# A reciprocal of 128 x 512 softmax denominators issued as two of 128 x 256, in a convolution and attention kernel

## The chip, the cores and the metric

The kernel runs on one core of one Trainium2 chip. The metric is the time of one execution on the device in microseconds (us). Four runs of the kernel before gave 3142.19, 3145.72, 3148.43 and 3150.03 us; their median is 3147.07 us.

## The reference, cut to what matters

The input x has four images of 128 channels and 64 x 64 pixels, in f32. Layer 0 adds to x the output of a block that normalises x in groups of channels, sums three convolutions (7x7, 5x5, 3x3), adds a non-local attention and applies a ReLU. Layer 1 reads the pixels as 4096 tokens per image, adds a state-space mixer that runs forwards and backwards over the tokens, and then a recurrence with a sigmoid. Only the attention of layer 0 is touched:

```python
g_x = conv1x1(x, gw, gb).reshape(B, IC, hw)
theta = conv1x1(x, tw, tb).reshape(B, IC, hw)
phi = conv1x1(x, pw, pb).reshape(B, IC, hw)
f = jnp.einsum('bcn,bcm->bnm', theta, phi) / jnp.sqrt(jnp.float32(IC))
attn = jax.nn.softmax(f, axis=-1)
out = jnp.einsum('bcm,bnm->bcn', g_x, attn)
```

IC is 64 and hw is 4096. The softmax needs, for each of the 4096 queries n, the sum over all keys of exp(f). The kernel divides by that sum at the end, on the output.

## The kernel before, in words

The activations stay in one tile `t` of 128 channels x 16384 pixels in SBUF. Layer 0 (`conv_attention`) goes through 32 query tiles of 512 pixels, eight for each image, in one loop over n (L627). It fills roughly the first 1660 us of the span; the mixer and the recurrence of layer 1 fill the rest.

One query tile has two parts. In the first, an inner loop (L639) goes eight times over four blocks of keys. `scores` (L454) multiplies keys and queries on TensorE into PSUM (`pf`) and takes the exponential on ScalarE (`ex`, L462). `values` (L466) multiplies the exponentials with the values into a PSUM tile `acc` (L471), and VectorE adds the exponentials up into the SBUF tile `es` (L475, L477). Behind the loop L651 folds the two halves of `es` into one of 512 columns.

In the second part the generator `convolve` (L375) does the tile's share of the convolutions. It multiplies transformed pixels `yf` with transformed weights `wt` or `wc` on TensorE (`products`, L355, matmuls at L367), four or six groups one after the other, each into a PSUM tile `pm`. VectorE and ScalarE combine them (L410 to L420), GpSimd adds them further (L426, L432, L433, L437, L438 and `put`, L380) and makes the next pixels (`transform` and `forms`: L298, L337, L347). At the second yield of `convolve` the loop calls `divide` (L479): a matmul with a matrix of ones (L481) sums `es` over the partitions, so that all 128 rows of the PSUM tile `den` hold the 512 denominators; VectorE takes the reciprocal into the SBUF tile `att` (L483), notes its largest and smallest value (L484, L485, from one partition) and multiplies `acc` with it (L486). Between these steps the loop issues `queries` for the next tile (L449), and in the last tile of an image the `keys` of the next image (L259). `collect` (L489) projects `att` and adds it to `t`.

Three PSUM buffers under the tag "c" are shared by everything small: `pm`, `den`, `pt` (queries), `pc` (collect), `pp`, `pg` and `gt` (keys). A new tile under this tag waits until the last reader of the tile that held its buffer is done. In most tiles of the loop a `pm` two places behind `den` takes over the buffer of `den`, and so its first matmul waits for L483.

The order on TensorE and ScalarE is the order in which the program is written (L232). The order on VectorE, GpSimd and the transfer queues is set by a scheduler that works with estimated durations. In the built program a reciprocal is followed on VectorE by L484 and L485, in some tiles with one L414 ahead of them; nothing stands between L483 and what it waits for, the matmul L481.

A reciprocal of another size occurs once more in the code that runs, at L1042 in the mixer: 128 x 256 from SBUF to SBUF.

Of the kernel before, what the change touches and what calls it, by code (L numbers as in the profile page):

```python
# [17 lines left out]
NC = 512  # L18
# [135 lines left out]
def conv_attention(nc, tc, k, a, t, B, H, W, flags, load, mem, loads):  # L154
# [32 lines left out]
    with ExitStack() as ctx:  # L187
# [291 lines left out]
        def divide(n, acc, es):  # L479
            den = ps_c.tile([P, NC], F32, tag="c", name="den")  # L480
            nc.tensor.matmul(den, k.ones, es[:, 0, :], start=True, stop=True)  # L481
            att = wk.tile([P, NC], F32, tag="att", name="att", bufs=4)
            nc.vector.reciprocal(att, den)  # L483
            nc.vector.tensor_reduce(dmax[:, n : n + 1], att[0:1, :], AX.X, ALU.max)  # L484
            nc.vector.tensor_reduce(dmin[:, n : n + 1], att[0:1, :], AX.X, ALU.min)  # L485
            nc.vector.tensor_tensor(att, acc, att, ALU.mult)  # L486
            return att
# [139 lines left out]
        for n in range(N):  # L627
# [25 lines left out]
            for i, _ in enumerate(convolve(n, b, m, f, wts)):  # L653
# [9 lines left out]
                if i == 1:  # L663
                    atts[n] = divide(n, acc, es)
# [1089 lines left out]
```

## Time and profile before

| what | value |
|---|---|
| median of four runs | 3147.07 us |
| the profiled execution's own time | 3142.8 us |
| its span | 3141.1 us (1.7 us lie around it) |
| granted TensorE clock, mean over the span | 0.981 |
| TensorE busy, 500 to 900 us | 389.58 of 400 us |
| VectorE busy, 500 to 900 us | 276.20 of 400 us |
| GpSimd busy, 500 to 900 us | 243.77 of 400 us |
| ScalarE busy, 500 to 900 us | 169.56 of 400 us |
| reciprocal L483 | 32 times, 107.4 us in all |

The page of the profile lists busy time by engine, the span in 40 slices, the chain of work that ended last, and groups of equal instructions with the idle time of their engine ahead of them. PE is TensorE, PEld its weight loads, DVE VectorE, ACT ScalarE, POOL GpSimd, SP the queue of the transfers. A wait is written as who waited, an arrow, and who ended the wait.

### The profile page before, as it was taken

Reading aid. Unit: us, or ns where it says so; the run is one execution under the profiler, and the core shown is the slowest. Engines: PE = TensorE matmul, PEld = TensorE weight load, DVE = VectorE, ACT = ScalarE, POOL = GpSimd, SP = SyncE. Lnnn points to the kernel's source line nnn. Section 1 sums busy time; section 2 is a strip of 40 time slices with the busy share of each in tenths; the row PEclk is TensorE's granted clock in tenths of the full one; section 3 lists DMA queues with packets and bytes.
Section 4 is the critical chain, followed back from the end, with each engine's and each line's share of the span. In section 5 each row is a group of like instructions: output and inputs, shape, how many; then the busy total and the mean of one; then the engine's idle time right before and its main releaser. Section 6 shows DMA issues by size and latency. Waiting matters only on the chain. (4 is left out here: it accounts for less than half of the span.)

```text
span 3141.1 us, 42863 instructions
## 1 busy us (share of the span) xinstructions
PE 2936.4 (93%) x15511; PEld 1458.3 (46%) x15511; DVE 2197.1 (70%) x3429; ACT 1815.6 (58%) x3102; POOL 1803.8 (57%) x1394
## 2 busy tenths in 40 slices
PE   6899999999999999999997999999999999999976
PEld 2345444454444454444453444444444444455545
DVE  7876668666677667677765767677677767677667
ACT  3343334434344433444434878887788778888756
POOL 4258448456584655766552565555555665555644
PEclk9999999999999999999998999999999999999988
DMA  5310101010100101011023343334333343334332
GB/s 182 133 40 29 38 31 45 8 44 23 46 23 30 43 23 38 31 53 36 8 80 88 95 115 92 98 95 115 85 99 92 90 110 98 95 98 101 87 109 109
DMA packets 108394, 224.16 MB, mean 71 GB/s; under 512 B 25678, under 2 KB 29390, under 8 KB 106764
## 3 DMA queue, kind: packets, MB, share of 16 engines
q1 hardware_dynamic: 96588, 177.53, 20.2%
q10 hardware_dynamic: 11584, 43.78, 4.1%
q8 instruction: 125, 2.05, 0.3%
q14 instruction: 97, 0.79, 0.1%
HBM read 200.83 MB, written 20.44 MB: 70 GB/s over the span
## 5 line engine op out<-in xcount | busy, mean ns | idle before, releaser
L477 DVE TENSOR_TENSOR es<-es,ex 128x1024 f32<-128x1024 f32 x448 | 685.3, 1530 | 133.6 <-ACT ex L462 100.0
L462 ACT ACTIVATE ex<-pf 128x1024 f32<-128x1024 f32 x512 | 497.6, 1022 | 461.0 <-PE pf L460 418.1
L460 PE MATMUL pf<-theta,phi 64*128 64x512 f32 x2048 | 512.8, 618 | 20.4 <-ACT ex L462 19.9
L471 PE MATMUL acc<-ex,gT 128*64 128x512 f32 x2048 | 490.3, 605 | 1.7 <-ACT ex L462 1.7
L1202 POOL TENSOR_TENSOR ct<-ct,Cst 128x512 f32<-128x512 f32 x128 | 169.9, 1327 | 395.2 <-DMA ct<-csmem 372.8
L460 PEld LDWEIGHTS pf<-theta,phi 64*128 64x128 f32 x2048 | 173.0, 185 | 339.4 <-ACT ex L462 173.8
L1168 ACT ACTIVATE lt<-lt,cs 128x128 f32<-128x128 f32 x1024 | 312.2, 390 | 0.5 <-DMA lt<-csmem 0.5
L367 PE MATMUL pm<-yf,wt 128*128 128x256 f32 x1152 | 287.1, 382 | 11.9 <-DVE att L483 11.0
L410 ACT ACTIVATE eo<-pm 128x256 f32<-128x256 f32 x88 | 33.8, 384 | 448.7 <-PE pm L367 442.2
L471 PEld LDWEIGHTS acc<-ex,gT 128*64 128x64 f32 x2048 | 127.2, 136 | 337.6 <-issue 325.7
L367 PEld LDWEIGHTS pm<-yf,wt 128*128 128x128 f32 x1152 | 212.9, 189 | 93.4 <-issue 38.7
L1103 PE MATMUL pb<-tl,wbc_fwd 128*64 128x512 f32 x512 | 237.6, 607 | 2.8 <-DVE xT L1135 2.8
L1103 PE MATMUL pb<-tl,wbc_bwd 128*64 128x512 f32 x512 | 238.2, 607 | 0.0
L337 POOL TENSOR_TENSOR yf<-yd 128x272 f32<-128x272 f32 x192 | 236.0, 1257 | 1.4
L1267 POOL TENSOR_TENSOR yT<-yT,zT 128x512 f32<-128x512 f32 x127 | 170.3, 1349 | 35.7 <-DVE yT L1254 32.9
L337 POOL TENSOR_TENSOR yf<-xp 128x272 f32<-128x272 f32 x128 | 108.8, 881 | 129.7 <-PE pm L367 123.9
L1201 DVE TENSOR_TENSOR lt<-lt,gm 128x1024 f32<-128x1024 f32 x128 | 178.9, 1398 | 1.9
L1135 DVE SCALAR_TENSOR_TENSOR xT<-px,taps_bwd,xT 128x512 f32<-128x512 f32 x192 | 143.8, 749 | 8.9 <-ACT xT L1129 4.0
L1234 PE MATMUL y<-lt,xdt 128*64 128x128 f32 x2048 | 141.2, 280 | 4.4 <-PE ptr L1177 4.0
L1103 PEld LDWEIGHTS pb<-tl,wbc_fwd 128*64 128x64 f32 x512 | 65.8, 138 | 164.2 <-issue 137.4
L1221 POOL TENSOR_TENSOR S<-S,tot 128x256 f32<-128x256 f32 x120 | 91.3, 761 | 84.7 <-PE y L1242 83.2
L367 PE MATMUL pm<-yf,wc 128*128 128x256 f32 x512 | 131.2, 384 | 6.6 <-DVE att L483 5.1
(297 smaller groups left out, 5678.3 us busy)
## 6 DMA issues: line engine op xcount, KB each, us to landing
lt<-csmem SPq DMA_DIRECT2D x128, 512.0 KB, 5.7
wt<-wd ACTq DMA_DIRECT2D x72, 576.0 KB, 3.8
ct<-csmem SPq DMA_DIRECT2D x256, 128.0 KB, 5.3
rs<-m SPq DMA_DIRECT2D x31, 512.0 KB, 3.6
wd<-t SPq DMA_DIRECT2D x16, 576.0 KB, 2.8
t<-in_x SPq DMA_DIRECT2D x4, 2048.0 KB, 10.9
rows<-after SPq DMA_DIRECT2D x32, 256.0 KB, 4.8
out<-t SPq DMA_DIRECT2D x4, 2048.0 KB, 14.4
```

What stands on the lines that cost most here:

```text
L337: nc.gpsimd.tensor_tensor(f[:, kx], at(x), at(y), op)
L367: nc.tensor.matmul(pm[:, e, :], wt, src, start=(i == 0), stop=(i == len(terms) - 1))
L460: nc.tensor.matmul(pf[:, e, :], phi[HALF[e], m, :], th[HALF[e]], start=True, stop=True)
L462: nc.scalar.activation(ex, pf, AF.Exp, scale=scale)
L471: nc.tensor.matmul(acc[HALF[e]], gT[:, 2 * m + e, :], ex[:, e, :], start=(m == 0), stop=(m == NT // 2 - 1))
L477: nc.vector.tensor_tensor(es, es, ex, ALU.add)
L1103: nc.tensor.matmul(out, w[i]["bc"][:, tap, bass.ts(c, DS)], src, start=(tap == 0), stop=(tap == KC - 1),)
L1135: nc.vector.scalar_tensor_tensor(at(n), px, taps[:, PAD - n : KC - n], at(n), ALU.mult, ALU.add)
L1168: nc.scalar.activation(v, v, AF.Relu, scale=-1.0, bias=m["b"]["cs"][:, d, m["i"], h : h + 1])
L1201: nc.vector.tensor_tensor(lt, lt, gm.unsqueeze(2).to_broadcast([P, ND, NHEAD, P]), ALU.mult)
L1202: nc.gpsimd.tensor_tensor(m["ct"], m["ct"], Cs[:, cols].unsqueeze(1).to_broadcast([P, NHEAD, P]), ALU.mult)
L1267: eng.tensor_tensor(v, v, gr["z"][d][:, :, half(d, j // 2)], ALU.mult)
```

## The change

The one reciprocal of 128 x 512 becomes two of 128 x 256, over the left and the right half of the columns. Everything else in the source is as it was.

```diff
             den = ps_c.tile([P, NC], F32, tag="c", name="den")
             nc.tensor.matmul(den, k.ones, es[:, 0, :], start=True, stop=True)
             att = wk.tile([P, NC], F32, tag="att", name="att", bufs=4)
-            nc.vector.reciprocal(att, den)
+
+            for i in range(2):
+                nc.vector.reciprocal(att[:, bass.ts(i, NC // 2)], den[:, bass.ts(i, NC // 2)])
             nc.vector.tensor_reduce(dmax[:, n : n + 1], att[0:1, :], AX.X, ALU.max)
             nc.vector.tensor_reduce(dmin[:, n : n + 1], att[0:1, :], AX.X, ALU.min)
             nc.vector.tensor_tensor(att, acc, att, ALU.mult)
```

In the built program the order of the instructions on VectorE, TensorE, ScalarE and the transfer queues is otherwise the same; the two halves stand one behind the other, and the second has no wait of its own. On GpSimd five additions L426 change places with the L347 behind them, one L337 moves ahead by a few places, and one small L74 moves by one. On TensorE 26 first matmuls of a `pm` now wait for two things, VectorE and TensorE's own earlier matmul `den`; one instruction holds one of these waits, so that 25 waiting instructions (event semaphores) are new on its queue.

## The prediction

> **What bounds the kernel now.** I read the page first, its busy times and its 40 slices. Each slice is 78.5 us, so slices 2 to 21 are the loop over the 32 query tiles, in which the change lies.
>
> ```profile
> PE 2936.4 (93%) x15511; PEld 1458.3 (46%) x15511; DVE 2197.1 (70%) x3429; ACT 1815.6 (58%) x3102; POOL 1803.8 (57%) x1394
> ...
> PE   6899999999999999999997999999999999999976
> ...
> DVE  7876668666677667677765767677677767677667
> ```
>
> TensorE (PE) is busy over nine tenths of nearly every slice of the loop, VectorE (DVE) six or seven. The loop goes at TensorE's pace, and VectorE counts only where TensorE stands still for it. So the second view is the list of waits of TensorE alone from 96 to 1650 us; its columns are the total in us, the count, and the longest.
>
> ```profile
> PE pm L367 <- DVE att L483: 16.1, 19, 0.8
> PE pf L460 <- ACT ex L462: 11.7, 33, 1.8
> PE gt L280 <- ACT g L276: 8.5, 12, 0.9
> ```
>
> The largest wait in the list is the one on the reciprocal: 19 tiles, 16.1 / 19 = 0.85 us each. The third view, the timeline of one such tile, shows what it is.
>
> ```profile
> 141.91 1.02 PE L481 MATMUL den<-es,ones 128*128 128x512 f32 x2
> ...
> 142.96 3.36 DVE L483 RECIPROCAL att<-den 128x512 f32<-128x512 f32 x1 [0.17 <-PE den L481]
> ...
> 144.49 1.04 PE L449 MATMUL pt<-xp,tw 128*128 128x512 f32 x2
> ...
> 146.24 0.36 DVE L414 SCALAR_TENSOR_TENSOR eo<-pm,eo 128x256 f32<-128x256 f32 x1
> 146.38 0.73 PEld L367 LDWEIGHTS pm<-yf,wc 128*128 128x128 f32 x4 [1.70 <-DVE att L483]
> 146.38 1.13 PE L367 MATMUL pm<-yf,wc 128*128 128x256 f32 x4 [0.85 <-DVE att L483]
> ...
> 149.34 0.69 DVE L418 TENSOR_TENSOR eo<-eo,pm 128x512 f32<-128x512 f32 x1 [0.64 <-PE pm L367]
> ```
>
> The reciprocal ends at 142.96 + 3.36 = 146.32; the matmul that takes over the PSUM buffer of `den` starts at 146.38, 0.06 later. So in 19 tiles the path runs from `den` through the whole reciprocal back to TensorE, and each ns by which the reciprocal ends later is lost. What it delays on VectorE itself is covered: at 149.34 VectorE sits 0.64 us waiting for TensorE.
>
> In the other 13 tiles TensorE does not wait for L483. In eight of them each `pm` group has eight matmuls and not four, and TensorE comes to the buffer later: in the tile at 285.74 the reciprocal ends at 289.10 and the weight load of the next `pm` starts at 289.44, a cover of 289.44 - 289.10 - 0.06 = 0.28 us. In three (448.85, 851.70, 1254.89) a weight load for L267 waits 0.33 us for L485 behind the reciprocal. The first tile (96.14) waits for ScalarE afterwards, and the tile at 1502.85 for nothing of VectorE.
>
> **What the change removes, adds and moves.** It removes 32 reciprocals of 128 x 512 and adds 64 of 128 x 256. Nobody can start earlier: L484, L485 and L486 read all 512 columns, and the buffer of `den` is free only when both halves have been read. So there is no gain in the source; it is a matter of what the split costs. The groups by form give both sizes:
>
> ```profile
> L483 DVE RECIPROCAL att<-den 128x512 f32<-128x512 f32 x32 | 107.4, 3358 | 5.8 <-PE den L481 5.7
> L1042 DVE RECIPROCAL u<-u 128x256 f32<-128x256 f32 x4 | 7.0, 1747 | 1.8 <-ACT xe L1041 1.8
> ```
>
> Half the columns take 1747 ns and not 1679: the line through both rows is 3358 - 1747 = 1611 ns for 256 columns plus a fixed 1747 - 1611 = 136 ns. L1042 reads SBUF and L483 PSUM. The nearest row for a PSUM source is L246, a copy of one column, at 158 ns in all; with that as the fixed part a half is (3358 - 158) / 2 + 158 = 1758 ns. I take 1747.
>
> Between two halves there may be overlap. The second waits for nothing; how VectorE runs two such instructions is seen in the mixer, L1135, alternating between two tiles that do not depend on each other, and in the tile above:
>
> ```profile
> 1703.87 0.74 DVE L1135 SCALAR_TENSOR_TENSOR xT<-px,taps_fwd,xT 128x512 f32<-128x512 f32 x1
> 1704.53 0.74 DVE L1135 SCALAR_TENSOR_TENSOR xT<-px,taps_bwd,xT 128x512 f32<-128x512 f32 x1
> ```
>
> The second starts 0.66 us after the first, which lasts 0.74: 0.08 us overlap. L414 at 146.24 starts 0.08 ahead of the end of the reciprocal as well, so a reciprocal in front allows it. Where the second does depend on the first, it starts about 0.04 later than its end (L1042 ends at 1691.06 + 1.75 = 1692.81, L1043 starts at 1692.85).
>
> - Reciprocal, as I take it: 2 x 1.747 - 0.08 - 3.358 = **+0.056 us** a tile. Lower bound: no fixed part at all and overlap, 2 x 1.679 - 0.08 - 3.358 = -0.08. Upper bound: fixed part of L246 and no overlap, 2 x 1.758 + 0.04 - 3.358 = +0.198.
> - TensorE's queue: in the built program the `pm` that waits for L483 now has two conditions, VectorE and its own earlier matmul `den`. The second is long met (`den` has ended before the reciprocal starts), but the VectorE condition now stands in a waiting instruction of its own ahead of the matmul: 26 more at L367 and one fewer at L83. The rows of L367 list 102 such instructions, 51 ns at the least and in the median. Where the wait ends the idle time that is **+0.051 us**. Lower bound 0 (the queue covers it); upper bound 0.051 plus a second restart of 0.06 as above, 0.11.
> - GpSimd: five L426 and the L347 behind them change places (in the runs before at about 194, 514, 917, 1320 and 1415 us). L426 comes 1.2 us later, L347 1.2 us earlier. No wait of TensorE for GpSimd is in its list, and the results of L426 there are read by L432 or L437 a tile later. I take 0; if that cover were gone it is 1.2 us each way, five times.
>
> Sum on the path: 19 x (0.056 + 0.051) = **+2.0 us**. The eight tiles with eight matmuls hide 0.11 behind their 0.28 us, and the three with `keys` lose at most 3 x 0.1. The profiled execution took 3142.8 us (span 3141.1), so its counterpart is 3144.8. It is 4.3 us below the median of the four runs, and the loss is one of fixed durations, so it goes on the median: 3147.07 + 2.0 = 3149.1, predicted **3149**.
>
> [...]
>
> **The rivals.**
>
> - *Slower, by an exposed second half.* The second reciprocal starts only when the first is out of the pipeline, its start-up is that of a PSUM read, and TensorE restarts twice: 0.198 + 0.11 = 0.308 us a tile. With the three `keys` tiles that is 22 x 0.308 = 6.8 us: 3153.9, +0.22%. It decides from 6.3 / 22 = 0.29 us a tile. For it: two reciprocals in a row are nowhere in the trace. Against it: the overlap behind L483 itself.
> - *Nothing lost.* The halves cost 1.68 each and overlap, and the queue hides its wait: between 19 x (-0.08) = -1.5 and 0 us, 3145.6 to 3147.1. Against it: L1042 at 1747.
> - *Faster, through GpSimd.* With L347 earlier the next pixels `yf` are ready earlier. If each of five L347 and the one L337 that moves were on the path, it is 6 x 1.2 = 7.2 us: 3139.9, -0.23%. Against it: TensorE's waits name no GpSimd, and GpSimd itself waits 123.9 us for TensorE to free `yf`.
> - *The change does not do what it says.* The halves stand as two instructions in the built program, so this falls out.
>
> **How the numbers follow.** The forecast gets 0.64, nothing lost 0.20, the slower rival 0.10, the faster one 0.06. A measurement of this kernel can tell about 0.2%, 6.3 us, from no change; the first two cases lie within that: same 0.84, slower 0.10, faster 0.06. The range takes in the first three cases, 3145.6 to 3153.9, and 2 us at each side for the median of a few runs that lie between 3142.2 and 3150.0: 3143.5 to 3156.
>
> **What would show it.** Right: 64 rows of L483 near 1747 ns, the second starting 0.08 us ahead of the first one's end; TensorE's wait for L483 still in 19 tiles, at about 0.96 us each, 18 us in all; 128 waiting instructions at L367. Wrong: halves well over 1.76 us or a gap between them; a TensorE wait of over 1.1 us, or one in the eight-matmul tiles; a new wait of TensorE for `yf` or `eo` of GpSimd.

## The result and the profile after

The changed kernel takes 3150.36 us (median of 35 runs, 3145.02 to 3158.01), the kernel before 3146.82 us beside it (57 runs, 3139.31 to 3154.43). The ratio is 1.0013, with a 95% interval of 1.0008 to 1.0018: 4.1 us slower, between 2.5 and 5.7 (the two medians lie 3.5 us apart). That is within 0.2%, as forecast, and on the side that was forecast; against these runs the sum of 2.0 us was too small. A repetition in another set of runs (e1 below) gave 1.0003, 0.9994 to 1.0013, which is 0.9 us and does not exclude 0 or 2.0 us.

The groups by form of the kernel after show the two halves, 107.8 us in all where the one reciprocal took 107.4. The view of L485 shows that the 64 are of two kinds (columns: shortest, median, longest, in ns).

```profile
L485 DVE RECIPROCAL att<-den 128x256 f32<-128x256 f32 x64 | 107.8, 1726 | 5.8 <-PE den L481 5.7
```

```profile
L485 DVE RECIPROCAL att<-den x64: 1694/1726/1759, 96.5 to 1649.6; 128x256 f32<-128x256 f32 x64
```

The timeline, asked for each half of the tile shown before by itself, says which is which:

```profile
143.18 1.76 DVE L485 RECIPROCAL att<-den 128x256 f32<-128x256 f32 x1 [0.17 <-PE den L481]
```

```profile
144.85 1.70 DVE L485 RECIPROCAL att<-den 128x256 f32<-128x256 f32 x1
```

The first half takes 1759 ns, the second 1694, and the timeline gives 3.37 us for both together. So the second starts 1.759 + 1.694 - 3.37 = 0.08 us ahead of the end of the first, as forecast, and is itself 0.065 us shorter. TensorE's list of waits, again from 96 to 1650 us:

```profile
PE pm L367 <- DVE att L485: 18.1, 19, 1.0
PE pf L460 <- ACT ex L462: 12.2, 33, 2.3
PE gt L280 <- ACT g L276: 8.5, 12, 0.9
PE pv L252 <- DVE qv L250: 4.6, 3, 1.6
```

The same 19 tiles wait, 18.1 us and not 16.1, the very figure that was forecast; but the timeline of the tile shown before has it from another place:

```profile
143.18 3.37 DVE L485 RECIPROCAL att<-den 128x256 f32<-128x256 f32 x2 [0.17 <-PE den L481]
...
146.47 0.36 DVE L414 SCALAR_TENSOR_TENSOR eo<-pm,eo 128x256 f32<-128x256 f32 x1
146.67 0.73 PEld L367 LDWEIGHTS pm<-yf,wc 128*128 128x128 f32 x4 [1.77 <-PE pt L449]
146.70 1.10 PE L367 MATMUL pm<-yf,wc 128*128 128x256 f32 x4 [0.95 <-DVE att L485]
```

The second half ends at 143.18 + 3.37 = 146.55. The weight load starts at 146.67 and the matmul at 146.70: 0.12 to 0.15 us later, where the kernel before took 0.06. The rows of L367 name what is new there, 128 waiting instructions now (first row) and 102 before (second row):

```profile
L367 PEldq EVENT_SEMAPHORE  x128: 51/51/706, 77.8 to 1656.4; - x128
```

```profile
L367 PEldq EVENT_SEMAPHORE  x102: 51/51/705, 77.4 to 1653.5; - x102
```

How much of this reaches the end is read from the starts of the 32 reciprocals, before against after. From one tile to the next the difference grows by 0.07 to 0.09 us in 14 of the 19 waiting tiles and changes by 0.01 or less in most others. Four waiting tiles show no growth, and one holds the jump below; without that one the 19 add up to 1.0 us. The list of waits says 2.0 us, 0.105 a tile, because the first matmul, which starts 0.03 us after its weight load now, is shorter by as much (1.10 for 1.13).

At one place the difference jumps by 2.29 us, between the tiles that start at 1103.73 and 1148.75 in the profile before. There TensorE waits for the group statistics of the next image (L236): `pm` (L244), three small VectorE operations, `pv` (L252). The loop has three such places; TensorE's list of waits before has them as

```profile
PE pv L252 <- DVE qv L250: 4.1, 3, 1.6
```

At the jump, before:

```profile
1112.43 2.47 POOL L337 TENSOR_TENSOR yf<-yx 128x272 f32<-128x272 f32 x4
1112.79 0.16 DVE L246 COPY gm<-pm 128x1 f32<-128x1 f32 x1 [0.41 <-PE pm L244]
1112.98 0.16 DVE L248 TENSOR_TENSOR dm<-mv,gm 128x1 f32<-128x1 f32 x1
...
1113.85 0.35 PE L252 MATMUL pv<-qv,gmean 128*128 128x1 f32 x2 [1.10 <-DVE qv L250]
...
1114.13 1.99 PE L460 MATMUL pf<-theta,phi 64*128 64x512 f32 x8
```

and after:

```profile
1113.30 2.46 POOL L337 TENSOR_TENSOR yf<-yx 128x272 f32<-128x272 f32 x4
...
1113.73 0.16 DVE L246 COPY gm<-pm 128x1 f32<-128x1 f32 x1 [0.48 <-PE pm L244]
1113.92 0.66 DVE L248 TENSOR_TENSOR dm<-mv,gm 128x1 f32<-128x1 f32 x1
...
1115.33 0.35 PE L252 MATMUL pv<-qv,gmean 128*128 128x1 f32 x2 [1.63 <-DVE qv L250]
...
1115.61 3.68 PE L460 MATMUL pf<-theta,phi 64*128 64x512 f32 x8
```

Two things are to be seen. L248 starts 0.55 us after GpSimd's first L337 before, and 0.62 us after it now, just where the second L337 begins (one lasts 0.65 and overlaps the next by 0.03 to 0.04); it takes 0.66 us instead of 0.16. The profiles of before, after and e1 to e3 agree with that: where GpSimd's L337 or L347 ran when L248 started, L248 took 0.48 to 0.66 us and ended 0.01 to 0.02 us after it, 12 times; where that operation had 0.08 to 0.10 us left, three times, as in the kernel before at this place, L248 took its 0.16. So one shift of 0.07 us, TensorE's against GpSimd's, becomes 0.5. (At the second statistics it works the other way: L248 starts 0.06 us later into the same L337 and takes 0.48 us instead of 0.54.) And the eight matmuls behind it take 3.68 us, where they take 1.99 in the kernel before. The view of stretches gives the granted clock there (third figure from the end, PEclk; behind it stand the DMA share and the rate):

```profile
1115.60:1119.20 3.60, 3.60 (x9) 1.10 (x8) 2.79 (x3) 1.02 (x1) 3.60 (x4) 0.53 0.01 2
```

In the kernel before the same work has

```profile
1114.10:1117.70 3.60, 3.60 (x17) 1.19 (x17) 3.07 (x3) 1.94 (x2) 3.60 (x4) 1.00 0.01 2
```

A clock of 0.53 over 3.6 us loses 3.6 x 0.47 = 1.7 us; with the longer standstill, 1.63 - 1.10 = 0.53, that is the jump. Sum of the loop: 1.0 + 2.3 = 3.3 us, inside the interval of 2.5 to 5.7; from the first reciprocal to the last the two profiles differ by 3.1 us. The spans of the two profiled executions differ by 8.9 us, 3150.0 against 3141.1; the rest lies almost all behind the loop, where executions of one kernel differ by as much (theory C below).

### The profile page after: what moved, and what is told of

It reads as the page before. It is cut to its first block, busy times and chain, and to the rows that moved or that the text cites. A ratio compares the mean times of both kernels' runs of the same rounds, so it can differ in the third digit from the quotient of the medians.

```text
span 3150.0 us, 42920 instructions
## 1 busy us (share of the span) xinstructions
PE 2941.1 (93%) x15511; PEld 1460.6 (46%) x15511; DVE 2197.3 (70%) x3461; ACT 1815.7 (58%) x3102; POOL 1799.7 (57%) x1394
## 5 line engine op out<-in xcount | busy, mean ns | idle before, releaser
L477 DVE TENSOR_TENSOR es<-es,ex 128x1024 f32<-128x1024 f32 x448 | 680.3, 1518 | 140.4 <-ACT ex L462 107.8
L367 PE MATMUL pm<-yf,wt 128*128 128x256 f32 x1152 | 286.8, 381 | 12.7 <-DVE att L485 12.4
L367 PEld LDWEIGHTS pm<-yf,wt 128*128 128x128 f32 x1152 | 212.9, 189 | 93.7 <-issue 36.4
L337 POOL TENSOR_TENSOR yf<-yd 128x272 f32<-128x272 f32 x192 | 235.2, 1253 | 1.0
L337 POOL TENSOR_TENSOR yf<-xp 128x272 f32<-128x272 f32 x128 | 109.4, 886 | 134.3 <-PE pm L367 128.5
L367 PE MATMUL pm<-yf,wc 128*128 128x256 f32 x512 | 131.1, 384 | 7.3 <-DVE att L485 5.7
```

Of the source, the lines that this page charges most:

```text
L337: nc.gpsimd.tensor_tensor(f[:, kx], at(x), at(y), op)
L367: nc.tensor.matmul(pm[:, e, :], wt, src, start=(i == 0), stop=(i == len(terms) - 1))
L477: nc.vector.tensor_tensor(es, es, ex, ALU.add)
```

## The experiments

The theories were: A, the loss is the waiting instruction on TensorE's queue; B, the split itself costs on VectorE; C, something outside the loop pays for the longer programs; from the second set on also D, the half-rate steps behind the statistics.

**e1, the change again.** No edit.

> The changed kernel once more, as the yardstick of this call. In its trace TensorE restarts 0.12 to 0.15 us after the end of the second half, where the kernel before took 0.06, and the pair of halves takes 3.37 us, where the one reciprocal took 3.36. Theory A (the loss is the waiting instruction on TensorE's queue, about 0.075 us in each of the 19 tiles): the starts of the tiles drift by 1.4 us over the loop, TensorE's wait for the reciprocal is about 18 us in all, and the time is 1.0005 to 1.0018 of the kernel before. Theory B (the split itself costs on VectorE): the same time, but it must come from the 3.37 us, which gives 19 x 0.015 = 0.3 us only. Theory C (57 more instructions shift the programs, and something outside the loop pays): a loss of 2 us or more that the starts of the tiles do not show.

Measured: 3148.32 us against 3147.12, ratio 1.0003 (0.9994 to 1.0013). Pair of halves 3.37 us, wait 18.1 us in 19 tiles, drift 0.07 a tile in 14 of them, 1.0 us where A expects 1.4. But the starts of the tiles also jump three times, by 1.66, 1.66 and 2.25 us, all at the statistics. This was not foreseen, and theory D came from it.

**e2, the matmul `den` in two, one reciprocal.** The edit is shown against the changed kernel.

```diff
-            nc.tensor.matmul(den, k.ones, es[:, 0, :], start=True, stop=True)
+            for i in range(2):
+                h = bass.ts(i, NC // 2)
+                nc.tensor.matmul(den[:, h], k.ones, es[:, 0, h], start=True, stop=True)
-            for i in range(2):
-                nc.vector.reciprocal(att[:, bass.ts(i, NC // 2)], den[:, bass.ts(i, NC // 2)])
+            nc.vector.reciprocal(att, den)
```

> The matmul den is issued as two of 256 columns, the reciprocal is one of 512. Base for the next run. The matmuls of pm show four passes of 256 columns in 1.02 us and den two passes of 512 in 1.02 us, so TensorE's work should not change: A, B and C all expect 0.9995 to 1.0010 of the kernel before, TensorE's wait for the reciprocal 16 us in 19 tiles, a restart 0.06 us after it.

Measured: 3147.40 us, ratio 1.0005 (0.9995 to 1.0014); wait 16.1 us in 19 tiles, restart 0.06, no drift. It is a clean base for the waiting tiles; at the first two statistics its tile starts jump by 1.67 and 1.66 us, as in e1.

**e3, the matmul `den` in two and the reciprocal in two.** As e2, with the two halves of the change kept.

> The matmul den in two and the reciprocal in two halves. In this build the pm that takes over the buffer of den waits for VectorE alone again, directly and not through a waiting instruction. Theory A: the loss of the change is gone; restart 0.06 us after the second half, TensorE's wait 19 x 0.865 = 16.4 us, tile starts drift by 0.3 us against the run with one reciprocal, ratio within 0.0005 of that run. Theory B: the halves cost here what they cost in the change, so 1.4 us or more above the run with one reciprocal, TensorE's wait 18 us. Theory C: the 32 reciprocals more shift VectorE's program as in the change, so a loss without drift.

Measured: 3147.25 us, ratio 1.0003 (0.9995 to 1.0012). The list of waits, the waiting instructions at L367 and the tile of before:

```profile
PE pm L367 <- DVE att L487: 16.3, 19, 0.9
```

```profile
L367 PEldq EVENT_SEMAPHORE  x101: 51/51/697, 77.5 to 1653.1; - x101
```

```profile
142.88 3.37 DVE L487 RECIPROCAL att<-den 128x256 f32<-128x256 f32 x2 [0.17 <-PE den L484]
...
146.31 0.73 PEld L367 LDWEIGHTS pm<-yf,wc 128*128 128x128 f32 x4 [1.71 <-DVE att L487]
146.31 1.13 PE L367 MATMUL pm<-yf,wc 128*128 128x256 f32 x4 [0.86 <-DVE att L487]
```

The halves end at 146.25 and TensorE starts at 146.31, 0.06 later. The drift is 0.01 to 0.03 us a tile. So the split itself costs about 0.01 us in a tile, (16.3 - 16.1) / 19, and the rest of the 0.07 goes with the waiting instruction: A holds and B falls, shown by the traces; the medians alone could not tell 1 us. In the third statistics TensorE stands still 1.09 us here, with no step.

**e4, `den` copied by ScalarE.** One reciprocal, in SBUF; the edit is shown against the changed kernel.

```diff
-            for i in range(2):
-                nc.vector.reciprocal(att[:, bass.ts(i, NC // 2)], den[:, bass.ts(i, NC // 2)])
+            nc.scalar.copy(att, den)
+            nc.vector.reciprocal(att, att)
```

> ScalarE copies den to att in SBUF and the one reciprocal works there in place, so that the buffer of den is free after a copy of about 0.6 us and not after 3.36. If the 0.85 us in 19 tiles are the path, as the prediction said, TensorE's wait of 16.1 us goes: 3147 - 16 = 3131 us, ratio 0.995. Rival: the reciprocal starts 0.75 us later, L418 behind it is late by as much, and TensorE waits there or for the copy instead, so the ratio is 0.998 to 1.001.

Measured: 3134.75 us, ratio 0.9957 (0.9944 to 0.9970), 13.5 us faster than the kernel before. TensorE's wait for the reciprocal is gone from the list. That the 0.85 us of 19 tiles were the path is so confirmed; some 3 us less than the 16 came out, with longer standstills at the second and third statistics (1.97 and 2.22 us), half the rate behind all three (the eight matmuls of `pf` in 3.66, 3.67 and 3.35 us, for 1.99), and small new waits for `wt` (2.7 us in eight) in its place.

**e5, the statistics of the kernel before in three steps.** `statistics` becomes a generator that yields ahead of L243 and ahead of L251 and is advanced at i = 1, 3 and 5 of the inner loop.

```diff
-                gn[b + 1] = statistics(b + 1)
+            counting = statistics(b + 1) if b + 1 < B and q == NQ - 3 else iter(())
...
                 values(i, exs, acc, es)
+                if i in (1, 3, 5):
+                    next(counting, None)
```

> The kernel before with the group statistics of the next image (L236) taken in three steps of the inner loop and not in one go: TensorE has matmuls of scores and values between the two small matmuls of L244 and L252, and no longer waits there. Theory D: in three of the 32 tiles TensorE stood still up to 1.6 us for L250, and in some executions ran at half its rate behind it for about 3.5 us, which cost a step of 1.66 us each time (none of three in the profile of before, one in that of the change, three in its repetition); this is a share of the spread between runs, and of the gap between the two medians. It expects the wait of 4.1 us and all steps gone, 4 to 9 us, ratio 0.9971 to 0.9987, and no step of over 0.5 us between the starts of the tiles. Rival: the steps come from elsewhere and stay, ratio 0.9985 to 1.

Measured: 3142.62 us against 3147.52, ratio 0.9992 (0.9982 to 1.0001). TensorE's wait at L252 is gone from its list, and the loop is 3.1 us shorter than in the profile of before, at just these three places (1.22, 1.12 and 0.76); no step is left. The ratio is a miss on the weak side, 0.9992 where 0.9971 to 0.9987 was expected: part of that range is in its interval, and so is 1.

**e6, the change with the same edit.**

> The changed kernel with the same edit. With the half-rate steps gone from both, what is left between this and e5 should be the waiting instructions alone: 19 x 0.075 = 1.4 us by theory A, ratio to e5 1.0005, and it should show as a drift of 0.07 us in each of 19 tiles. Theory C (something outside the loop pays) expects 3 us or more between the two, and a longer stretch behind 1660 us.

Measured: 3142.12 us, ratio 0.9987 (0.9976 to 0.9998). Against e5 the starts of the tiles drift by 0.07 to 0.09 us in 17 of the 19 waiting tiles, 1.37 us over the loop, and jump nowhere. The medians of e5 and e6 lie 0.5 us apart, the other way; a loss of 1.4 us is below what they tell. Without the standstills at the statistics the change loses in the trace only what A says.

**e7, the copy and the statistics in three steps.** Both edits together.

> Both edits that help: the copy of den by ScalarE (0.9957) and the statistics in three steps. If the two waits lie in different places of the path they add up: 0.9957 - 0.0013 to 0.0029, so 0.993 to 0.9944, 3125 to 3129 us. Rival: ScalarE or VectorE becomes the bound in the tiles with statistics, and it stays at 0.9957.

Measured: 3128.90 us, ratio 0.9952 (0.9939 to 0.9964). It is the fastest of all versions run here, 18.6 us below the median of before in the same set; the gains add up in the medians. The ratio is a miss, 0.9952 where 0.993 to 0.9944 was expected; it fits the sum of what e4 and e5 measured (0.9957 - 0.0008), and the intervals of e4 and e7 overlap, so that it does not exclude the rival either. Its profile has one step of 1.78 us; TensorE's list of waits has 1.9 us ahead of `pc`, as in e4.

**e8, the reciprocal in four.** `range(4)` and `NC // 4`.

> The reciprocal in four pieces of 128 columns. TensorE's waiting instructions are those of the change. If a start-up of 136 ns hides behind the piece in front except for 15 ns, as the two halves showed (1694 + 1759 ns, 3.37 us together), the four take 3.36 + 3 x 0.015 = 3.40 us, TensorE's wait grows to 19 x 0.985 = 18.7 us and the tile starts drift by 0.105 us in each of the 19 tiles. If the start-up of each piece were paid, 3 x 0.056 = 0.17 us come on top of 3.36: 3.53 us, 21 us of waits.

Measured: 3151.52 us in one execution. The waits:

```profile
PE pm L367 <- DVE att L484: 18.5, 19, 1.0
```

The drift is 0.09 to 0.11 us in 15 of the 19 waiting tiles, 0.02 to 0.03 more than with two halves, close to what two more starts of 15 ns would give. At the first two statistics the tile starts jump by 1.66 us each. At the third TensorE stands still 1.61 us, and the step is 0.60 us, without the half rate.

**e9 to e12, one more execution each of the kernel before, the change, the kernel before and the change.**

> The kernel before, one more profiled execution, to count where TensorE runs at half its rate behind the statistics of L252 (three places, in the tiles 4, 12 and 20, each seen as a step of about 1.66 us between the starts of the tiles). Theory D: the steps fall by chance, more often where TensorE has stood still for 1.6 us ahead of L252 than for 1.1; in the third place the kernel before stood still for 1.10 us and the change for 1.63. It expects here no step in the third place and some in the first two, so fewer than in the changed kernel. Rival: as many steps in both, and the third place as long.

> The changed kernel, one more profiled execution for the same count. Theory D: a standstill of 1.63 us in the third place again (0.54 more than before), with the half rate behind it in most executions; drift of 0.07 us in each of 19 tiles. Rival: as in the kernel before.

> As e9, a second execution: the same standstills (1.57, 1.44 and 1.10 us), the steps by chance.

> As e10, a second execution: the same standstills (1.58, 1.38 and 1.63 us), the steps by chance.

Measured: 3152.43, 3149.93, 3150.95 and 3148.54 us, single executions, which say nothing of a difference of 4 us. The count, with the first profiles and e1 (growth of the difference between the starts of the tiles, against the first profile of before; "standstill" is the wait ahead of L252):

| place | kernel before (3 profiles) | changed kernel (4 profiles) |
|---|---|---|
| first, standstill | 1.57 in all | 1.57 to 1.58 |
| first, steps of about 1.66 us | 1 of 3 | 2 of 4 |
| second, standstill | 1.44 in all | 1.37 to 1.38 |
| second, steps of about 1.66 us | 2 of 3 | 2 of 4 |
| third, standstill | 1.10 in all | 1.63 in all |
| third, step | 0 of 3 | 4 of 4: 2.29, 2.25, 2.24, 2.28 |

In the first two places the steps come in some executions and not in others, in both kernels alike. At the third the longer standstill belongs to the change, in four of four profiles. The half rate came behind it each time, but e8 stood still for 1.61 us there and its eight matmuls of `pf` took 1.99 us, so four of four is no rule. One more step, 0.59 us in e10, lies a tile ahead of the first place.

On theory C: from the last reciprocal to the end of the span the kernel before takes 1496.7, 1504.2 and 1501.1 us, the changed kernel 1502.1, 1498.1, 1501.7 and 1497.2. The stretch behind the loop varies by over 7 us between executions and is not longer after the change. Nothing here speaks for C; but a loss of 1 or 2 us there would not show in seven profiles that spread so far.

## Why the prediction was right, and what in its sum was not

- **TensorE sets the pace and the reciprocal's end is on the path in 19 tiles**: right. The same 19 tiles wait in every run that keeps the order, and taking the wait away (e4) is worth 13.5 us.
- **Nobody can start earlier**: right for the readers of `att` and of the buffer. Elsewhere some waits of TensorE became a little shorter (at the second statistics 1.37 us for 1.44).
- **The reciprocal, +0.056 us a tile**: too much; about 0.01, from 3.37 against 3.36 and from e3. The overlap is the forecast 0.08 us. The length of the halves was not: the line through L483 and L1042 gave 1747 ns for each, and the first takes 1759, the second, behind another reciprocal, 1694.
- **The waiting instruction, +0.051 us**: the right place, a little too small; the restart grew from 0.06 to 0.12, so +0.06. It lies between the bounds, which ended at 0.11.
- **Their sum, 19 x 0.107 = 2.0 us**: 1.0 us on the path in the first pair of profiles, 1.4 between e5 and e6, 0.07 a tile where it shows. The list of waits shows the forecast 18 us, but 0.03 us a tile, 0.6 in all, of them is the weight load, which now starts ahead of the matmul. That the 18 us came true was in part luck: the restart of the matmul grew by 0.09 us, more than was forecast, and the reciprocal by less.
- **GpSimd, "I take 0"**: this step missed 2.25 us. TensorE's list names no GpSimd after the change either, as assumed; but the drift of 0.07 us moved VectorE's L248 against GpSimd's L337 by just the margin that it had, 0.53 us of standstill came of it, and behind it TensorE's granted clock was 0.53 over 3.6 us. The prediction looked for who waits for GpSimd and not for who runs beside it. The list of waits of before had the place: `pv` waited three times, up to 1.57 us.
- **The rivals**: the exposed second half would have shown 0.2 us more on VectorE; it shows 0.01. "Nothing lost" falls with the drift in the traces and with the first set of runs (the repetition alone would not exclude it), and no gain came through GpSimd.

The total of 3.3 us that the traces show, and the 4.1 that the runs show, lie in the range. The path and the waiting instruction were foreseen; that 2.0 us lies so near is in part luck, since the terms that were foreseen came to 1.0 to 1.4 us and the larger part is a place that the prediction took at nothing.

## What to carry to other kernels

A split has a price also where its two parts run back to back: it can change what the next user of the buffer waits for, and here a second, long met condition cost some 0.06 us a tile, several times the 0.01 of the split itself. Read the built program's waits, not only its order. If the reader of a shared PSUM buffer is slow, move the data out with an idle engine rather than split the slow reader: in e4 the buffer of `den` was read by a copy of 0.59 us and not by the reciprocal of 3.36, which was worth 13.5 us. And when a change shifts one engine by some hundredths of a microsecond, look for the places where the bounding engine stands still for over one: here a shift of 0.07 us became 2.29 at such a place.

## What the runs showed of the hardware that was not expected

TensorE ran at half its rate after standstills of 1.37 to 1.63 us, and not in each execution: 11 of 18 such places in the profiles of the two kernels (before three times, the change four times), counting the third place of the change, and none of the three at 1.10 us in the kernel before. The granted clock was 0.53 over 3.6 us at the third place of the first profile, and the steps show a loss of about 1.7 us each time.

The length of the standstill alone does not decide. The eleven profiles that have standstills ahead of L252 have 33 of them. Behind 18, all of 1.36 us or more, the eight matmuls of `pf` took 2.47 to 3.68 us; behind the other 15 they took 1.99, and of these five lasted 1.08 to 1.10 us and ten 1.37 to 1.61.

The profiles before and after also show where the granted clock changes. Before, it is 0.50 just ahead of 98.05 us, 1.00 from there to 1668.18, and 0.50 behind it: 1570.13 us, which is 460 times 3.413. After the change it rises to 1.00 at 98.58, is 0.50 from 1115.76 to 1119.17, and falls to 0.50 again at 1672.13: 298, 1 and 162 times 3.413 us. Here are two neighbouring stretches of this length in the profile after at the third statistics, and two at the first (the edge at 306.80 is counted back from 1115.76, 237 times 3.413 us):

```profile
1112.35:1115.76 3.41, 1.78 (x12) 0.94 (x10) 2.29 (x11) 1.94 (x2) 3.33 (x6) 1.00 0.00 0
1115.76:1119.17 3.41, 3.41 (x8) 0.94 (x8) 2.72 (x3) 1.02 (x1) 3.41 (x4) 0.50 0.01 2
```

```profile
303.38:306.80 3.42, 3.32 (x15) 1.55 (x13) 0.76 (x2) 1.23 (x2) 3.42 (x6) 1.00 0.00 0
306.80:310.21 3.41, 1.94 (x10) 0.98 (x10) 3.17 (x6) 1.19 (x2) 3.41 (x5) 1.00 0.00 0
```

At the third statistics the standstill of 1.63 us ends at 1115.33, inside the first stretch and 0.43 us ahead of its end, and the second runs at half rate. At the first, the 1.58 us from 306.69 to 308.27 go over the edge at 306.80, and there is no half rate. Counted in the same way, an estimate, the 1.38 us at the second statistics go over an edge too (709.57), as do the 1.44 us of the kernel before (709.04), and its 1.57 us begin 0.09 us behind one (306.27); none of the three was followed by the half rate. So the place against these edges may be what makes the same standstill cost in one execution and not in the next. Five places in two profiles do not show that, and no run was made to test it.
